# When the accumulator of the first graph layer is zeroed, which engine empties the table's products, and how many buffers that stage has

## The chip, the cores and the metric

The kernel runs on one core of one Trainium2 chip. The core has five engines that run side by side, each with its own queue of instructions: TensorE (PE in the profile, with its weight loads as PEld), VectorE (DVE), ScalarE (ACT), GpSimd (POOL) and SyncE (SP), which mostly issues transfers. ACT, SP and POOL issue DMAs. The time is that of one execution on the device in microseconds (us). Before the change the median of 11 runs is 4143.52 us (4135.31 to 4149.55). The time wanted is the median after the change.

## The reference

Four layers run on a graph with 6250 nodes of 256 features and 100000 edges, sorted by destination: a graph attention block (two attention layers), a mixture of experts, a graph layer with weighted means, and a second mixture of experts. Only the opening of the first attention layer matters here:

```python
x = x + _L0_gnn_ref(_layernorm(x, axis=-1), src, dst, ...)
# gat_layer, first call: 2 heads of 128
z = (x @ W).reshape(num_nodes, heads, d)
el = jnp.einsum('nhd,hd->nh', z, a_l)
er = jnp.einsum('nhd,hd->nh', z, a_r)
...
s = jax.ops.segment_sum(ex, dst, num_segments=num_nodes)
alpha = ex / s[dst]
msg = z[src] * alpha[:, :, None]
out = jax.ops.segment_sum(msg, dst, num_segments=num_nodes)
```

## The kernel before, in words

The 6250 nodes are 50 tiles of 125. A layer on the graph takes the tiles in turn: for each of a tile's 16 groups of 128 edges it gathers the sources' rows from a table in DRAM (`z<-table,src_all`, line 755, an indirect DMA on POOL), and TensorE adds them up by destination (line 946). Sums that belong to edges beyond a tile's 16 groups go through an accumulator in DRAM, `sums1` for the first layer: a few "over" groups are added up first and written to its rows (lines 741 to 748), and each tile adds the rows that it finds there (`old<-sums`, line 663). So `sums1` has to be zero before any of this: 6528 rows of 258 floats, 1032 bytes each, 6.74 MB.

The first stage, lines 1145 to 1184, prepares all that, and the change lies in it. It has these parts, in the order of the program:

- `edge_ranges` (lines 124 to 407) finds where each tile's edges begin and end. It is one chain with three rounds of indirect loads on POOL: the whole edge list is loaded and reduced, then `part` (line 177, 50 rows of 6256 bytes), then `win` (line 220, three loads of 50 rows of 1024 bytes), from which VectorE makes `wd` (line 226), then `orec` and `ow` (line 293, eight loads of 128 small records). Between the rounds stand dozens of small VectorE instructions and small matmuls into a `p` buffer of PSUM, two of which exist. At its end `starts` (line 383) and `shift_held` (line 407) are there.
- `edge_lists` (lines 441 to 499) reads `starts` into registers of SP and POOL and loads each tile's edges and weights in 7 groups of 8 tiles (lines 460 and 463; two buffers), turns them on TensorE and stores them in the lists that the gathers use.
- `gat_weights` prepares `wl`, the layer's weights.
- A loop makes the table in 13 blocks of up to four tiles (lines 1151 to 1173): load `xb` on ACT's queue (three buffers), layer norm on VectorE, turn on TensorE (line 523) and copy on ScalarE (line 524), then per tile four matmul instructions into `pz` (line 1164, two buffers of PSUM). Two engines empty a `pz`: ScalarE its 256 columns of z (line 1168), VectorE its 4 columns of scores (line 1171). Then the rows (two buffers) are stored on ACT's queue (line 1106).
- Some blank rows are stored, `sums1` is zeroed by one DMA on SP's queue from a blank SBUF tile of 128 partitions (`clear`, line 1120), and `item_lists` (lines 409 to 433) makes the list for a loop that handles irregular tiles.

No `manual_schedule` stands around this stage. The framework's scheduler chooses the order in which each engine gets these instructions, from the program's order and its own estimates, and puts the waits in. So an instruction that is ready early is issued early although it stands late in the program: the zeroing of `sums1`, nearly the last line of the stage, is issued 10.93 us after the start. Within an engine the order is then fixed, and an instruction that waits holds all behind it.

After the stage comes the loop for irregular tiles, with a run-time count (line 651); all engines meet there. The first gather of the layer is issued at 169.33 us, and from there the order is written out by hand (lines 967 to 1015).

Of the kernel before, what the change touches and what calls it, by code (L numbers as in the profile page):

```python
# [13 lines left out]
F32 = mybir.dt.float32  # L14
# [4 lines left out]
OP = mybir.AluOpType  # L19
# [8 lines left out]
P = 128  # L28
NP = 125
D = 256  # L30
# [4 lines left out]
TB = 4  # L35
# [9 lines left out]
def network(ctx: ExitStack, tc: tile.TileContext, a, out, n_nodes: int, n_edges: int):  # L45


    nc = tc.nc
    NT = a["x"].shape[0] // NP
# [71 lines left out]
        return t  # L121


    def edge_ranges():

# [1 line left out]
        with tc.tile_pool(name="rng", bufs=1) as pool, tc.tile_pool(  # L129
            name="rng_ps", bufs=2, space=PSUM  # L130
# [60 lines left out]
            p = ps.tile([P, 512], F32, name="p")  # L191
# [32 lines left out]
                )  # L224
            wd = pool.tile([NT, 3 * P], F32, name="wd")
            nc.vector.tensor_copy(wd, win.rearrange("p i e k -> p (i e) k")[:, :, 1])
            nc.vector.tensor_scalar(c(18), c(18), float(P), None, op0=OP.add)
            upper = pool.tile([NT, 3 * P], F32, name="upper")
            nc.vector.scalar_tensor_tensor(
# [9 lines left out]
            p = ps.tile([P, 512], F32, name="p")  # L239
# [7 lines left out]
            p = ps.tile([P, 512], F32, name="p")  # L247
# [20 lines left out]
            p = ps.tile([P, 512], F32, name="p")  # L268
# [50 lines left out]
            p = ps.tile([P, 512], F32, name="p")  # L319
# [6 lines left out]
            p = ps.tile([P, 512], F32, name="p")  # L326
# [20 lines left out]
            p = ps.tile([P, 512], F32, name="p")  # L347
# [22 lines left out]
            p = ps.tile([P, 512], F32, name="p")  # L370
# [10 lines left out]
            p = ps.tile([P, 512], F32, name="p")  # L381
            nc.tensor.matmul(p[:1, :NT], c(5), identf[:NT, :NT], start=True, stop=True)
            nc.vector.tensor_copy(starts, p[:1, :NT])
            p = ps.tile([P, 512], F32, name="p")
# [117 lines left out]
    def normalize(pool, outs, ins, keep=None):  # L502

        n, p = len(ins), ins[0].shape[0]
        mv = keep if keep is not None else pool.tile([P, TB, 2], F32, name="mv")
        for j, x in enumerate(ins):
            st = pool.tile([P, 6], F32, name="st", bufs=4)
            nc.vector.bn_stats(st[:p], x)
            nc.vector.bn_aggr(mv[:p, j, :], st[:p])
        nc.scalar.activation(mv[:p, :n, 1:2], mv[:p, :n, 1:2], AF.Sqrt, bias=eps[:p])  # L510
        nc.vector.reciprocal(mv[:p, :n, 1:2], mv[:p, :n, 1:2])
        for j, (o, x) in enumerate(zip(outs, ins)):
            nc.vector.tensor_scalar(
                o, x, mv[:p, j, 0:1], mv[:p, j, 1:2], op0=OP.subtract, op1=OP.mult
            )

    def transpose_to(xT, ps, ins, func=AF.Copy):

        n, q = len(ins), ins[0].shape[0]
        for k in range(KD):  # L520
            pt = ps.tile([P, TB, P], F32, name="pt")
            for j, x in enumerate(ins):
                nc.tensor.transpose(pt[:, j, :q], x[:, k * P : (k + 1) * P], identf[:q, :q])
            nc.scalar.activation(
                xT[:, k, : n * q].rearrange("p (j q) -> p j q", q=q), pt[:, :n, :q], func
            )


    def gat_width(H):
        return H * (D // H + 1)  # L530

    def gat_weights(pool, W, al, ar, H):

        d = D // H
        wl = pool.tile([P, KD, D + 2 * H], F32, name="wl")
        nc.sync.dma_start(wl[:, :, 0:D], W.rearrange("(k p) f -> p k f", p=P))
        for s, v in enumerate((al, ar)):
            vb = row_to_all(pool, v, f"vb{s}")
            for h in range(H):
                for k in range(KD):  # L540
                    pr = pool.tile([P, D], F32, name="pr", bufs=2)
                    nc.vector.tensor_mul(pr[:, :d], wl[:, k, h * d : (h + 1) * d], vb[:, h * d : (h + 1) * d])
                    nc.vector.tensor_reduce(
                        wl[:, k, D + s * H + h : D + s * H + h + 1], pr[:, :d], AX.X, OP.add
                    )
        return wl
# [550 lines left out]
    def tiles_of(src, t0, n):  # L1097

        w = src.shape[1]
        return bass.AP(tensor=src.tensor, offset=src.offset + t0 * NP * w, ap=[[w, P], [NP * w, n], [1, w]])  # L1100

    def store_tiles(queue, dst, t0, n, v):

        to = dst[t0 * NP : (t0 + n) * NP, :].rearrange("(j p) w -> p j w", p=NP)
        for q in (slice(0, NP // 16 * 16), slice(NP // 16 * 16, NP)):
            queue.dma_start(to[q], v[q])  # L1106
# [7 lines left out]
    def clear(queue, acc, part, parts):  # L1114

        w = acc.shape[1]
        step = -(-NS // parts)
        lo, hi = part * step, min(NS, (part + 1) * step)
        if lo < hi:
            queue.dma_start(  # L1120
                acc[:, :].rearrange("(p j) w -> p j w", p=P)[:, lo:hi, :],
                blank[:, 0:w].unsqueeze(1).to_broadcast([P, hi - lo, w]),
            )
# [12 lines left out]
    x5_d = dram.tile([NT * NP, D], F32, name="x5_d")  # L1136
    uv_d = dram.tile([NT * NP, 2 * D], F32, name="uv_d")
    x6_d = dram.tile([NT * NP, D], F32, name="x6_d")
    NS = -(-(NT * NP + 2 * P) // P)
    sums1 = dram.tile([NS * P, gat_width(2)], F32, name="sums1")  # L1140
    sums2 = dram.tile([NS * P, gat_width(1)], F32, name="sums2")
    sums3 = dram.tile([NS * P, D + 1], F32, name="sums3")


    with tc.tile_pool(name="g1w", bufs=1) as wpool, tc.tile_pool(name="g1", bufs=2) as work, tc.tile_pool(
        name="g1p", bufs=2, space=PSUM
    ) as ps:
        edge_ranges()
        edge_lists()
        wl = gat_weights(wpool, a["L0_gnn_W1"], a["L0_gnn_al1"], a["L0_gnn_ar1"], 2)  # L1150
        for t0, n in blocks:
            xb = work.tile([P, TB, D], F32, name="xb", bufs=3)
            nc.scalar.dma_start(xb[:, :n, :], tiles_of(a["x"], t0, n))
            xb = xb[:NP]
            normalize(work, [xb[:, j, :] for j in range(n)], [xb[:, j, :] for j in range(n)])
            xT = work.tile([P, KD, TB * NP], F32, name="xT")
            transpose_to(xT, ps, [xb[:, j, :] for j in range(n)])
            rows = work.tile([NP, TB, D + 6], F32, name="rows")
            heads = rows[:, :, 0 : D + 2].rearrange("p j (h f) -> p j h f", h=2)
            nc.vector.memset(heads[:, :, :, 0:1], 1.0)  # L1160
            for j in range(n):
                pz = ps.tile([P, 512], F32, name="pz")
                for k in range(KD):
                    nc.tensor.matmul(
                        pz[:NP, : D + 4], xT[:, k, j * NP : (j + 1) * NP], wl[:, k, :],
                        start=(k == 0), stop=(k == KD - 1),
                    )
                nc.scalar.copy(
                    heads[:, j, :, 1:], pz[:NP, 0:D].rearrange("p (h f) -> p h f", h=2)
                )  # L1170
                nc.vector.tensor_copy(rows[:, j, D + 2 :], pz[:NP, D : D + 4])
            nc.vector.tensor_copy(er1[:NP, t0 : t0 + n, :], rows[:, :n, D + 4 :])
            store_tiles(nc.scalar, table1, t0, n, rows[:, :n, :])
        none = wpool.tile([NT + 1, 2 * P], BF16, name="none")
        nc.vector.memset(none, 0.0)
        for v, k in ((er1_d, 6), (er2_d, 3)):
            nc.sync.dma_start(
                v[:, :, CH:, :].rearrange("t k c e -> t k (c e)"),
                none.unsqueeze(1).to_broadcast([NT + 1, k, 2 * P]),
            )  # L1180
        nc.sync.dma_start(x2_d[NT * NP :, :], blank[: P - NP, 0:D])
        nc.sync.dma_start(table3[NT * NP :, :], blank[: P - NP, 0 : D + 1])
        clear(nc.sync, sums1, 0, 1)
        item_lists()
    gat_general(2, table1, er1, sums1, m_all)

# [188 lines left out]
    with tc.tile_pool(name="f1w", bufs=1) as wpool, tc.tile_pool(name="f1x", bufs=3) as work, tc.tile_pool(  # L1375
        name="f1p", bufs=2, space=PSUM
# [17 lines left out]
        rows = wpool.tile([P, NC, 2], I32, name="rows")  # L1394
# [43 lines left out]
        p = ps.tile([P, 512], F32, name="py")  # L1438
# [3 lines left out]
        p = ps.tile([P, 512], F32, name="py")  # L1442
# [88 lines left out]
    with tc.tile_pool(name="f1c", bufs=2) as work:  # L1531
        for t0 in range(0, NT, TL):
# [8 lines left out]
            rows = work.tile([NP, TL, D + 1], F32, name="rows")  # L1541
# [383 lines left out]
    with tc.tile_pool(name="f3w", bufs=1) as wpool, tc.tile_pool(name="f3", bufs=1) as work, tc.tile_pool(  # L1925
        name="f3p", bufs=1, space=PSUM
# [51 lines left out]
```

## Time and profile before

| | us |
|---|---|
| median of 11 runs | 4143.52 |
| the profiled execution, its own time | 4141.28 |
| its span, first to last instruction | 4139.6 |
| first 168 us of it: PE busy | 103.36 |
| first 168 us: DVE busy | 100.09 |
| first 168 us: ACT busy | 41.00 |
| first 168 us: POOL busy | 41.25 |

The profile comes from one execution. The span leaves out 1.7 us of that execution's own time. In lines of the timeline the columns are the start in us, the duration in us, the engine (a q marks its queue, which issues DMAs), the line of the kernel, the operation, output and input, and the number of instructions; in brackets stands how long the engine sat idle before, and what ended that. The lines by window give each engine's busy us and number of instructions, the granted clock of TensorE, the mean busy share of the 16 DMA engines and GB/s.

### The profile page before, as it was taken

The page shows a single profiled execution, that of the slowest core. Times are in us where ns is not written, and L with a number is a line of the kernel's source. Part 1 is how long each engine was busy: PE and PEld are TensorE (multiplying, and loading weights), DVE is VectorE, ACT ScalarE, POOL GpSimd, SP SyncE. Part 2 cuts the span into 40 slices and gives each one's busy share as a digit, 9 for nine tenths or more (in the row PEclk, how much of TensorE's full clock was granted, in tenths as well). Part 3 has the DMA queues.
Part 4 walks back from the last instruction along what each step waited for, and adds up shares of the span by engine and source line. Part 5 has one row for each costly group of instructions (what it writes and reads, how often), then busy time and mean ns, then how long its engine had stood idle before and what let it go on. Part 6 is the DMA issues. An engine that isn't in the chain of part 4 may idle for free. (4 is left out here: it accounts for less than half of the span.)

```text
span 4139.6 us, 38013 instructions
## 1 busy us (share of the span) xinstructions
PE 2873.8 (69%) x11159; PEld 2004.7 (48%) x11159; DVE 2443.3 (59%) x4938; ACT 994.1 (24%) x1877; POOL 2614.8 (63%) x2717
## 2 busy tenths in 40 slices
PE   5556556666645666767667699990788888889854
PEld 3334434444433444444445477760346666666643
DVE  5666666666646777777777333336345445544474
ACT  1222222222212222223222122220011212222243
POOL 2477777777747777777776144440777777777611
PEclk8777878788777888888888699995678999989987
DMA  6445555555535555555554411128454544554644
GB/s 164 140 143 157 165 157 157 156 156 156 157 103 149 163 163 163 163 163 163 164 165 128 143 64 64 65 70 248 126 148 136 150 137 134 147 144 139 165 125 131
DMA packets 323716, 593.10 MB, mean 143 GB/s; under 512 B 64327, under 2 KB 210396, under 8 KB 323247
## 3 DMA queue, kind: packets, MB, share of 16 engines
q0 software_dynamic: 128432, 349.50, 30.2%
q1 hardware_dynamic: 177542, 223.76, 18.8%
q10 hardware_dynamic: 17529, 17.31, 1.4%
q8 instruction: 96, 1.57, 0.2%
q14 instruction: 117, 0.96, 0.1%
HBM read 489.23 MB, written 101.12 MB: 143 GB/s over the span
## 5 line engine op out<-in xcount | busy, mean ns | idle before, releaser
L755 POOL DMA_INDIRECT z<-table,src_all x2412 | 2330.3, 966 | 847.1 <-issue 797.7
L946 PE MATMUL pacc<-z,wt 128*125 128x258 f32 (+1 forms) x3216 | 950.1, 445 | 20.5 <-DVE old L956 17.6
L946 PEld LDWEIGHTS pacc<-z,wt 128*125 128x125 f32 x3216 | 680.0, 222 | 174.4 <-issue 26.2
L1075 PE MATMUL pacc<-z,wt 128*125 128x257 f32 x1608 | 490.9, 446 | 105.1 <-DMA z<-table,src_all 95.5
L895 PE MATMUL pq<-identf,el 128*34 128x128 f32 (+1 forms) x306 | 78.7, 391 | 668.1 <-ACT el L888 569.9
L1075 PEld LDWEIGHTS pacc<-z,wt 128*125 128x125 f32 x1608 | 312.2, 210 | 270.0 <-DMA z<-table,src_all 220.4
L765 DVE TENSOR_TENSOR oh<-iota_b,px 128x2000 bf16<-128x2000 bf16 x153 | 339.7, 2221 | 120.1 <-ACT px L1047 119.9
L895 PEld LDWEIGHTS pq<-identf,el 128*34 128x34 f32 (+1 forms) x306 | 26.4, 112 | 718.5 <-ACT el L888 645.4
L862 ACT CAST e<-pe 6x1536 bf16<-6x1536 f32 (+1 forms) x204 | 203.6, 998 | 688.8 <-PE pe L858 688.6
L934 DVE TENSOR_TENSOR z<-z,pq 128x1032 f32<-128x1032 f32 (+1 forms) x202 | 233.6, 1218 | 179.1 <-PE pq L918 175.6
L846 DVE TENSOR_TENSOR own<-dr,px 125x2048 bf16<-125x2048 bf16 x102 | 232.6, 2281 | 21.1 <-ACT px L844 13.0
L1759 PE MATMUL pt<-x6T,w1f 128*128 128x250 f32 x800 | 187.8, 392 | 69.0 <-ACT hT L1765 69.0
L1512 POOL DMA_INDIRECT y_d<-y,r x105 | 104.4, 994 | 197.6 <-DVE r L1456 171.1
L858 PE MATMUL pe<-own,ek 125*6 125x512 bf16 (+1 forms) x408 | 149.4, 457 | 101.1 <-DVE own L846 88.7
L1482 PE MATMUL ph<-w,xT 128*128 x420 | 201.2, 602 | 13.2 <-DVE xT L1471 7.3
L1759 PEld LDWEIGHTS pt<-x6T,w1f 128*128 128x128 f32 x800 | 157.2, 199 | 93.1 <-ACT hT L1765 74.9
L888 ACT COPY el<-z 128x32 f32<-128x32 f32 (+2 forms) x102 | 23.6, 231 | 739.5 <-DMA z<-table,src_all 716.0
L1506 PE MATMUL py<-w,hT 128*128 x840 | 198.5, 379 | 0.0
L1774 PE MATMUL py<-w2f,hT 128*125 128x256 f32 x800 | 189.4, 397 | 0.0
L899 DVE TENSOR_TENSOR_SCAN f<-mask,pq 34x384 f32<-34x384 bf16 (+1 forms) x100 | 93.8, 938 | 139.5 <-PE pq L895 139.3
L1774 PEld LDWEIGHTS py<-w2f,hT 128*125 128x125 f32 x800 | 159.7, 201 | 26.1
L1506 PEld LDWEIGHTS py<-w,hT 128*128 128x128 f32 x840 | 151.5, 190 | 16.3
(479 smaller groups left out, 3877.8 us busy)
## 6 DMA issues: line engine op xcount, KB each, us to landing
dr<-dl_d SPq DMA_DIRECT2D x102, 512.0 KB
z<-table,src_all POOLq DMA_INDIRECT x2412, 2.8
sums<-blank SPq DMA_DIRECT2D x16, 771.0 KB
uv_d<-uv SPq DMA_DIRECT2D x25, 448.0 KB
z<-uv_d SPq DMA_DIRECT2D x10, 1120.0 KB
old<-sums SPq DMA_DIRECT2D x13, 514.0 KB
sums<-blank SPq DMA_DIRECT2D x1, 6579.0 KB
old<-sums SPq DMA_DIRECT2D x10, 645.0 KB
```

The source lines that it names most:

```text
L755: nc.gpsimd.indirect_dma_start(out=z[:, c, :], out_offset=None, in_=table[:, :], in_offset=bass.IndirectOffsetOnAxis(ap=src_all[:, i : i + ...
L765: nc.vector.tensor_tensor(oh[:, c0:c1], iota_b[:, 0:NP].unsqueeze(1).to_broadcast([P, n, NP]), px[:, c0:c1].unsqueeze(2).to_broadcast([P, ...
L846: nc.vector.tensor_tensor(own, s["dr"][:NP], px[:NP, X : X + 1].to_broadcast([NP, CH * P]), OP.is_equal)
L858: nc.tensor.matmul(pe[:, c - lo : c - lo + n], ek[:, NT if t == OVER else t].rearrange("p i h -> p (i h)"), s["own"][:, c : c + n], start= ...
L862: nc.scalar.copy(s["e6"][:, lo:hi], pe[:, 0 : hi - lo])
L934: nc.vector.tensor_tensor(zz, zz, x.unsqueeze(2).to_broadcast([P, n, d + 1]), OP.mult)
L946: nc.tensor.matmul(s["pacc"][:NP, 0:w], s["wt"][:, c, :], s["z"][:, c, 0:w], start=(c == 0), stop=(c == n - 1),)
L1075: nc.tensor.matmul(pacc[:NP, 0:w], s["wt"][:, c, :], s["z"][:, c, :], start=(c == 0), stop=(c == chunks(t) - 1),)
L1482: nc.tensor.matmul(ph, v["xT"][:, k, :], w1[:, v["one"], k, :].rearrange("p o f -> p (o f)"), start=(k == 0), stop=(k == KD - 1),)
L1506: nc.tensor.matmul(py[:, :D], v["hT"][:, f, :], w2[:, v["one"], f, :].rearrange("p o f -> p (o f)"), start=(f == 0), stop=(f == KF - 1),)
L1759: nc.tensor.matmul(ph[:, g * W : (g + 1) * W], x["w1"][:, s, k, f * P : (f + 1) * P], xT[:, k, :], start=(k == 0), stop=(k == KD - 1),)
L1774: nc.tensor.matmul(py[:NP, s, :], hT[:, s * KF + f, :], x["w2"][:, s, f, :], start=(f == 0), stop=(f == KF - 1),)
```

## The change

`edge_ranges` gets a tile `zeros` of 48 partitions and 258 columns and fills it right after `wd`, by multiplying a part of `wd` with 0. One DMA on SP's queue stores it into all of `sums1`, each partition 136 times; the old zeroing at the end of the stage goes. As it reads `zeros`, this DMA can't be issued before `wd` is known. The 4 columns of scores in `pz` are copied by ScalarE where VectorE did it. The buffers of `xb` go from 3 to 5, those of `rows` from 2 to 3, those of `pz` from 2 to 3.

```diff
-    def edge_ranges():
+    def edge_ranges(zeros):
...
             nc.vector.tensor_copy(wd, win.rearrange("p i e k -> p (i e) k")[:, :, 1])
+            nc.vector.tensor_scalar(zeros, wd[:ZP, : zeros.shape[1]], 0.0, None, op0=OP.mult)
...
+    ZP = 48
     NS = -(-(NT * NP + 2 * P) // P)
+    assert NS * P % ZP == 0 and ZP <= NT
...
-        edge_ranges()
+        zeros = wpool.tile([ZP, gat_width(2)], F32, name="zeros")
+        edge_ranges(zeros)
+        rows_z = NS * P // ZP
+        nc.sync.dma_start(
+            sums1[:, :].rearrange("(p j) w -> p j w", p=ZP), zeros.unsqueeze(1).to_broadcast([ZP, rows_z, zeros.shape[1]])
+        )
         edge_lists()
...
-            xb = work.tile([P, TB, D], F32, name="xb", bufs=3)
+            xb = work.tile([P, TB, D], F32, name="xb", bufs=5)
...
-            rows = work.tile([NP, TB, D + 6], F32, name="rows")
+            rows = work.tile([NP, TB, D + 6], F32, name="rows", bufs=3)
...
-                pz = ps.tile([P, 512], F32, name="pz")
+                pz = ps.tile([P, 512], F32, name="pz", bufs=3)
...
-                nc.vector.tensor_copy(rows[:, j, D + 2 :], pz[:NP, D : D + 4])
+                nc.scalar.copy(rows[:, j, D + 2 :], pz[:NP, D : D + 4])
...
-        clear(nc.sync, sums1, 0, 1)
         item_lists()
```

## The prediction

> **What bounds the kernel now.** I first read the page's busy times, then the windows over the first 168 us, since only that stage changes, then its timeline and its waits.
>
> ```profile
> span 4139.6 us, 38013 instructions
> PE 2873.8 (69%) x11159; PEld 2004.7 (48%) x11159; DVE 2443.3 (59%) x4938; ACT 994.1 (24%) x1877; POOL 2614.8 (63%) x2717
> ...
> 0.00:168.00 168.00, 103.36 (x402) 69.74 (x402) 100.09 (x504) 41.00 (x112) 41.25 (x76) 0.85 0.55 142
> 168.00:4139.60 3971.60, 2770.42 (x10757) 1934.99 (x10757) 2343.16 (x4436) 953.12 (x1766) 2573.59 (x2641) 0.82 0.50 143
> ```
>
> In the first stage no engine is busy for two thirds of the time: PE leads with 103 of 168 us. So it is bound by waits. The other 3971.6 us are ordered by hand and untouched; I count them as unchanged. The timeline of the stage shows one chain from load to load:
>
> ```profile
> 10.93 0.65 SPq L1120 DMA_DIRECT2D sums<-blank  x1
> 15.59 26.10 SPq L1247 DMA_DIRECT2D y_d<-blank  x1
> 17.77 1.34 POOL L177 DMA_INDIRECT part<-in_edges,row  x1 [15.00 <-DVE wl L543]
> 29.17 0.56 DVE L183 CAST pd<-part 50x782 f32<-50x782 int32 x1 [7.09 <-DMA part<-in_edges,row]
> 35.72 0.93 POOL L220 DMA_INDIRECT win<-in_edges,near  x1 [16.61 <-DVE near L217]
> 44.32 0.43 DVE L508 BATCH_NORM_STATS2 st<-xb 125x6 f32<-125x256 f32 x1 [4.88 <-DMA xb<-in_x]
> 45.33 0.34 DVE L226 CAST wd<-win 50x384 f32<-50x384 int32 x1
> 57.91 0.17 DVE L276 COPY over<-p 128x12 f32<-128x12 f32 x1 [2.33 <-PE p L273]
> 60.45 0.97 POOL L293 DMA_INDIRECT orec<-in_edges,at_i  x1 [21.19 <-DVE sl L314]
> 72.54 0.17 DVE L299 TENSOR_SCALAR w_all<-ow 128x4 f32<-128x4 f32 x1 [0.40 <-DMA ow<-in_edge_weight,at_i]
> 84.90 6.76 SPq L460 DMA_DIRECT2D raw<-in_edges  x11
> 139.29 0.37 SPq L495 DMA_DIRECT2D run_d<-nb  x1
> 165.16 0.21 SPq L433 DMA_DIRECT2D item_off<-to  x1
> 169.33 0.97 POOL L755 DMA_INDIRECT z<-table,src_all  x1 [0.30 <-issue]
> ```
>
> The store of 6.74 MB of zeros goes out at 10.93, and the next DMA on SP takes 26.10 us to get past it. Right behind, `part` and `win` are asked for and come late: VectorE idles 7.09 us for the one and, around the other, 4.88 us for a block's `xb`. Then come `orec`, the first edge lists at 84.90, their last store at 139.29, the item lists until 165.16, the layer at 169.33. The DMA view of two windows, 11 to 46 us and 47 to 84 us, tells when the transfers are busy:
>
> ```profile
> DMA packets 8053, 8.34 MB, mean 238 GB/s; under 512 B 188, under 2 KB 7972, under 8 KB 8052
> q1 hardware_dynamic: 6705, 6.77, 89.9%
> ...
> DMA packets 3490, 3.21 MB, mean 87 GB/s; under 512 B 413, under 2 KB 3488, under 8 KB 3488
> ```
>
> SP's queue (q1) moves 6.77 MB in the first 35 us, so the store takes 35 us. In the next 37 us little is moved. The change shifts the store from the first window to the second.
>
> **The change part by part.** All sums are against the profiled execution's own 4141.28 us.
>
> *The store leaves the front.* `part` is issued at 17.77 and used at 29.17, 11.4 us later. Other indirect loads in this stage land 2.8 us (z, 2.1 MB in 16 loads), 3.6 us (`orec`) after issue by the DMA view. `part` is 0.31 MB in one load; I take at most 4.3 us, and then VectorE, busy until 22.07, doesn't wait: **-7.1** (from 0, if the two added `xb` loads of 0.5 MB take the store's place, to -7.1). The three loads of `win` land 6.7 us after issue by the same view; at 2.8 that is **-3.9**. For this the 4.88 us that VectorE waits for `xb` must go too: that load is issued only at 33.02, when a buffer comes free, and competes with the store; with five buffers it is issued among the first. Bounds 0 and -4.9.
>
> *The filling of `zeros`.* One VectorE instruction of 48x258 on the chain. The row of `wd` (50x384) is 0.34: **+0.3**.
>
> *The store in its new place.* It is issued when `wd` is known, at 45.33 + 0.34 + 0.3 - 11.0 = 35.0. The eight `orec` and `ow` loads then run beside it. They are on the chain (VectorE waits 4.83 and 0.40 us for them). `win` lost 3.9 us beside the same store; these move 128 records of 4 or 8 bytes each and are eight in a row of which the last counts. Bounds 0 and +3.9, I take **+2**. It ends at 35.0 + 0.65 + 35 = 70.6. What is queued behind the waiting store on SP: the register loads of `starts` and the edge lists' loads. They waited until 84.90 and come by this sum at 73.9, so there are 3 us between, and as the first group is used 6 us after its first load, 9 us of cover. `sums1` is read first near 239 us. The store's rate isn't known from 48 partitions. From 128 it is 6.74 MB / 35 us = 193 GB/s; were it proportional to the partitions, 72 GB/s and 93 us. I take 35, because the row has the same bytes in the same pieces of 1032 on the same queue.
>
> [...]
>
> *ScalarE empties `pz`.* VectorE loses 50 copies of 0.15, 7.2 us. ScalarE gains 50 copies; its nearest rows are 0.16 (128x16) and 0.20 (128x8), so 8 to 10 us on an engine that is busy for 41 of 168. On the path it matters that PE waits 18.3 us in 11 places for VectorE's copy before it may write `pz`, because VectorE has other work or a wait in front. One such place is on the chain: the matmul of line 273 stands behind those of `pz`, and VectorE waits 2.33 us for it: **-2.3** (0 to -2.3). Sum up to the edge lists: -7.1 - 3.9 + 0.3 + 2 - 2.3 = **-11.0**.
>
> *Five `xb`, three `rows`, three `pz`.* From 84 to 139 VectorE waits 2.69, 1.49 and 0.20 us for `xb`, with the edge lists' instructions behind it: **-3** (0 to -4.4). The rest of the 54 us goes by the lists' own loads, two buffers deep, and stays. From 139.29 to 165.16, 25.9 us, three and a half blocks of the table and the item lists remain, and PE is nearly full (19.2 of 20 us from 140 to 160). A block costs it 2 x 2.02 + 0.91 = 4.95 us. If blocks can run ahead in PE's and VectorE's earlier waits (18.3 and 14.6 us), fewer remain. I take one block: **-4.9** (0 to -9.9).
>
> Sum: -11.0 - 3 - 4.9 = **-18.9**, 4122.4 for an execution like the profiled one. The median of the runs shown is 2.2 us above that execution, so 4124.6; I say **4125**. All best ends give -28.3, 4115.
>
> **The rivals.** About 0.2%, 8.3 us, is what a measurement of this kernel can tell from no change.
>
> 1. *Only the chain moves.* The edge lists keep their pace, the blocks their place between them, the tail its 25.9 us. For it: the lists' waits are mostly for `raw` (9.1 us on ACT). -11.0, **4132.5**, and from 4129 to 4139 with the terms' ends.
> 2. *The table ends the stage, not the chain.* The 13 blocks are stored between 44.84 and 161.48, 9.7 us for each, and the last is 3.7 us before the last item list. If their pace is set by how the scheduler mixes them with the rest, what the chain gains is spent waiting. Against it: PE needs only 4.95 a block. **4142**, a few us to either side. It would also be seen if `part` came no earlier, the added `xb` loads having taken the store's place.
> 3. *The store stands before the edge lists (slower).* The lists' loads are on the same SP queue. With 48 partitions at a proportional rate the store lasts 93 us, to 128.7, and the first group comes near 130 where it was used at 90.9: +39, less the 3 and at most 9.9 of tail whose blocks are done meanwhile: about +26, **4170**. It costs from 44 us on (the 9 us of cover) and turns the sign near 63 us, 107 GB/s. Against it: the 193 GB/s row; for it: nothing in this trace stores much from so few partitions.
>
> **How the numbers follow.** Forecast 0.58, own range 4115 to 4135. Rival 1: 0.17, of it 0.12 faster and 0.05 within 0.2% (above 4135.2). Rival 2: 0.15, within. Rival 3: 0.07, slower; another 0.03 slower for an order of the scheduler's that puts a wait in front of the chain. So faster 0.70, same 0.20, slower 0.10. The range goes from 4112 (the best ends, and 3 us of spread between runs) to 4143, which takes in rival 1 and half of rival 2 and leaves out some 0.18.
>
> **What would show it.** VectorE's wait for `part` near zero and `pd` near 22; `wd` near 34; the store from 35 to 71, and SP's first load of edges near 74, landing without delay; PE's waits for line 1171 gone; the last edge list near 125, the last item list near 146, the first gather near 150. It is wrong if `part` still lands 11 us after issue, if the store lasts beyond 44 us, or if the stage's end stays while the edge lists begin earlier.

## The result, and the profile after

The changed kernel has a median of 4179.28 us in 8 runs (4174.76 to 4190.33); the kernel before, beside it on the same chip, 4144.69 us in 31. The ratio is 1.0087, with a 95% interval from 1.0077 to 1.0096: 0.87% slower, some 36 us by the ratio. The forecast was 4125 us, with a range up to 4143.

The profiled execution after has 4181.36 us of its own. Its page and two windows, cut at the end of the first stage (columns as before):

```profile
span 4179.5 us, 38019 instructions
...
0.00:208.80 208.80, 111.28 (x402) 72.65 (x402) 94.03 (x455) 45.62 (x162) 40.68 (x77) 0.73 0.45 114
208.80:4179.50 3970.70, 2775.74 (x10757) 1941.03 (x10757) 2343.36 (x4436) 953.62 (x1766) 2576.98 (x2641) 0.82 0.50 143
```

What comes after the stage takes 3970.7 us where it took 3971.6. All of the loss lies in the stage, 208.8 instead of 168 us, with hardly more work in it: VectorE is busy for 6 us less, ScalarE for 5 us more. The same places of the timeline after, up to the item lists' last store and the first gather:

```profile
17.84 1.34 POOL L178 DMA_INDIRECT part<-in_edges,row  x1 [15.07 <-DVE wl L545]
22.72 0.56 DVE L184 CAST pd<-part 50x782 f32<-50x782 int32 x1 [0.58 <-DMA part<-in_edges,row]
29.27 0.94 POOL L221 DMA_INDIRECT win<-in_edges,near  x1 [10.10 <-DVE near L218]
34.52 0.35 DVE L227 CAST wd<-win 50x384 f32<-50x384 int32 x1 [0.81 <-DMA win<-in_edges,near]
35.42 0.69 SPq L1155 DMA_DIRECT2D sums<-zeros  x1
42.67 5.73 ACTq L1108 DMA_DIRECT2D table<-rows  x2
47.42 0.97 POOL L295 DMA_INDIRECT orec<-in_edges,at_i  x1 [14.69 <-DVE sl L316]
68.31 0.18 DVE L511 BATCH_NORM_AGGREGATE mv<-st 125x2 f32<-125x6 f32 x1 [16.65 <-DMA table<-rows]
72.01 0.16 DVE L301 TENSOR_SCALAR w_all<-ow 128x4 f32<-128x4 f32 x1
89.54 0.18 DVE L513 RECIPROCAL mv<-mv 125x4 f32<-125x4 f32 x1 [8.41 <-DMA table<-rows]
89.87 0.40 ACTq L1162 DMA_DIRECT2D xb<-in_x  x1
90.76 0.37 ACT L1177 COPY rows<-pz 125x256 f32<-125x256 f32 x1 [14.05 <-PE p L355]
93.62 0.19 DVE L385 CAST starts<-p 1x50 int32<-1x50 f32 x1
96.14 4.49 POOL L465 DMA_DIRECT2D wraw<-in_edge_weight  x8 [39.00 <-PE pz L1173]
111.27 0.82 ACTq L1108 DMA_DIRECT2D table<-rows  x2
115.18 5.09 SPq L462 DMA_DIRECT2D raw<-in_edges  x3
180.04 0.31 SPq L497 DMA_DIRECT2D run_d<-nb  x1
205.94 0.21 SPq L435 DMA_DIRECT2D item_off<-to  x1
210.11 0.97 POOL L757 DMA_INDIRECT z<-table,src_all  x1 [0.30 <-issue]
```

Up to the first `orec` the chain gains 13.0 us (60.45 to 47.42). Then it loses. In us, from one place to the next:

| step | before | after | difference |
|---|---|---|---|
| start to first `orec` | 60.45 | 47.42 | -13.0 |
| to `starts` | 22.8 | 46.2 | +23.4 |
| to SP's first load of edges | 1.6 | 21.6 | +19.9 |
| to the lists' last store | 54.4 | 64.9 | +10.5 |
| to the first gather | 30.0 | 30.1 | 0 |
| sum | 169.33 | 210.11 | +40.8 |

Three kinds of wait are new, or far longer than before. The first: VectorE stands idle for 16.65 and 8.41 us until a *store of the table* has landed: its memset of a block's ones (line 1169) must not overwrite rows that are still being stored, and the program places that wait on the instruction just ahead. The store issued at 42.67 took 5.73 us to issue alone (0.87 before) and was waited for until 68.31. The second: SP's first load of edges waits, though `starts` is known. The waits of SP's queue from 96 to 136 us (us in total, times, longest) name the same transfers:

```profile
SPq L462 <- DMA table<-rows: 27.6, 3, 19.9
```

The loads read nothing that these stores write. The built program tells why they wait: the framework hands eight completion semaphores round among the DMAs of SP and ScalarE, and a DMA waits until the one that had its semaphore before it has landed (it *inherits* the semaphore). For the first load of edges that is the second store of the table's 7th block, issued at 111.27; before it was the 2nd block's first store.

The third wait is ScalarE's, 14.05 us up to 90.76. The view puts it down to a matmul, but by the built program the load of `xb` issued at 89.87, ahead of that copy in ScalarE's program, inherits the semaphore of the store of zeros itself. The trace's record of that semaphore has the store's last completion at 89.8. So ScalarE, and with it the table, stands until the whole store has landed. In the kernel before, that semaphore goes on to a store of the table issued after 61 us, and the zeros had landed at 48.8.

What makes the table's stores slow runs beside them. From 35 to 95 us the DMA view (the row's 40 slices of 1.5 us, then SP's queue) says of after:

```profile
DMA  7999999999999999999887779767665542210370
...
q1 hardware_dynamic: 6544, 6.74, 58.7%
```

The store isn't over in 35 us. It keeps the engines at nine tenths up to 63 us and then drains for over 20 us; by single us, the queue's last packets are near 89, so it lasted **54 us**. The row is a mean over the engines. That parts of the store end far apart the semaphore shows: its sixteen completions come between 63.5 and 89.8 us.

### The profile page after: what moved, and what is told of

Read it like the earlier page. It is cut to its first block, busy times and chain, and to the rows that moved or that the text cites. A ratio compares the mean times of both kernels' runs of the same rounds, so it can differ in the third digit from the quotient of the medians.

```text
span 4179.5 us, 38019 instructions
## 1 busy us (share of the span) xinstructions
PE 2887.0 (69%) x11159; PEld 2013.7 (48%) x11159; DVE 2437.4 (58%) x4889; ACT 999.2 (24%) x1927; POOL 2617.7 (63%) x2717
## 5 line engine op out<-in xcount | busy, mean ns | idle before, releaser
L1767 PEld LDWEIGHTS pt<-x6T,w1f 128*128 128x128 f32 x800 | 157.4, 200 | 94.3 <-ACT hT L1773 76.1
L890 ACT COPY el<-z 128x32 f32<-128x32 f32 (+2 forms) x102 | 23.6, 231 | 720.8 <-DMA z<-table,src_all 710.5
```

The costliest lines, as they stand in the source:

```text
L1767: nc.tensor.matmul(ph[:, g * W : (g + 1) * W], x["w1"][:, s, k, f * P : (f + 1) * P], xT[:, k, :], start=(k == 0), stop=(k == KD - 1),)
```

## The experiments

In the table "length" is the store's, from its issue to its queue's last packets; "blocks" is how many blocks of the table the scheduler put ahead of the first edge list in ScalarE's program; "waits for" names the transfer whose semaphore the first load of edges inherits (table's stores counted, two to a block); "hold" is the time from `starts` to that load; the last two columns are the profiled first gather and the ratio to the kernel before beside it. The kernels marked with * ran on two other chips, where TensorE's clock was granted at 0.77 instead of 0.82: their ratios compare, their first gathers only roughly. The profiled executions of e5, e10 and e13 are 27 to 39 us above the medians of their kernels.

| kernel | store | length | blocks | waits for | starts | hold | first gather | ratio (95%) |
|---|---|---|---|---|---|---|---|---|
| before | 128, front | 37 | 4 | store 3 | 83.3 | 1.6 | 169.3 | 1 |
| after | 48 | 54 | 9 | store 14 | 93.6 | 21.6 | 210.1 | 1.0087 (1.0077-1.0096) |
| e1_store_only | 48 | 51 | 9 | store 11 | 85.3 | 23.2 | 197.2 | 1.0059 (1.0038-1.0079) |
| e2_rest_only | 128, front | 44 | 4 | store 4 | 83.1 | 1.6 | 174.2 | 1.0005 (0.9994-1.0016) |
| e3_store_wide | 128 | 40 | 4 | store 4 | 78.2 | 2.0 | 165.8 | 0.9992 (0.9979-1.0005) |
| e4_store_late | 48, after lists | 52 | 4 | store 4 | 73.3 | 1.7 | 195.9 | 1.0062 (1.0041-1.0083) |
| e5_ones_once * | 48 | 52 | 9 | store 12 | 91.2 | 17.0 | 200.1 | 1.0042 (1.0020-1.0064) |
| e7_wide_ones * | 128 | 40 | 4 | a load of xb | 79.9 | 1.9 | 171.1 | 0.9986 (0.9967-1.0004) |
| e8_z64 * | 64 | 43 | 8 | store 7 | 79.2 | 6.5 | 184.6 | 1.0045 (1.0022-1.0069) |
| e9_z48_rows * | 48 | 52 | 9 | store 14 | 92.7 | 20.6 | 207.9 | 1.0083 (1.0056-1.0110) |
| e10_raw_pool * | 48 | 53 | 9 | (POOL) | 93.2 | 2.5 | 213.1 | 1.0058 (1.0032-1.0084) |
| e11_wide_only * | 128 | 42 | 4 | store 3 | 75.6 | 6.4 | 169.8 | 0.9977 (0.9959-0.9994) |
| e12_split * | 128, in three | | 4 | store 4 | 78.6 | 4.3 | 167.0 | 0.9983 (0.9967-1.0000) |
| e13_z32 * | 32 | 44 | 13 | a load of xb | 79.5 | 38.0 | 213.3 | 1.0048 (1.0030-1.0067) |
| e14_held | 48 | 52 | 4 | store of dl_d | 90.4 | 1.7 | 185.0 | 1.0039 (1.0025-1.0052) |
| e15_wide_late_lists | 128 | 40 | 8 | store 4 | 78.0 | 2.4 | 167.0 | 0.9989 (0.9980-0.9998) |

The diffs are against the changed kernel, that of e12 against the kernel before.

**e1_store_only**, the kernel before with only the store moved:

```diff
-            xb = work.tile([P, TB, D], F32, name="xb", bufs=5)
+            xb = work.tile([P, TB, D], F32, name="xb", bufs=3)
...
-                nc.scalar.copy(rows[:, j, D + 2 :], pz[:NP, D : D + 4])
+                nc.vector.tensor_copy(rows[:, j, D + 2 :], pz[:NP, D : D + 4])
```

(`rows` and `pz` go back too.)

> The kernel before with the store alone moved to its new place, from 48 partitions as in the change; buffers and VectorE's copies as before. Times are worked out from the two traces: before to after the first gather moved from 169.33 to 210.11, +40.8, of it -13.0 up to the first orec, +12.5 from there to starts known, wait on the table's stores included, +8.4 to 10.9 to the last of starts, +19.9 from starts to SP's first load of edges, +10.5 in the edge lists. Theory 1 (the long store alone does it: it slows the table's stores and xb, and VectorE and SP wait for them): nearly all of it stays, first gather 200 to 212, time 4170 to 4182. Theory 2 (the added buffers let more table stores go ahead of the edge lists, and SP's loads wait for those; the store only makes each longer): the 19.9 goes to a few us, first gather 180 to 192, time 4150 to 4165. Theory 3 (the copies and the buffers do it, the store is harmless): the front's gain of 11 to 13 alone is left, first gather near 157, time near 4130.

4169.46 us, +0.59%, first gather 197.2: just below both ranges of theory 1 and above those of theory 2. The store alone does most of it, and the hold of 23.2 us is there with the old buffers, against theory 2.

**e2_rest_only**, the change without the moved store:

```diff
-            nc.vector.tensor_scalar(zeros, wd[:ZP, : zeros.shape[1]], 0.0, None, op0=OP.mult)
...
+        clear(nc.sync, sums1, 0, 1)
         item_lists()
```

> The change without the moved store: zeros from 128 partitions at the very front as in the kernel before, with ScalarE's copies and the added buffers. Theory 1 (the moved store does it all): no loss, the front as before with part 11 us late; what the buffers and copies give by the prediction's terms is -2.3, -3 and -4.9, so 4131 to 4141. Theory 2 (buffers put table stores ahead of the edge lists and that alone costs): the step from starts to SP's first load is still 10 to 20 us instead of 1.6, time 4150 to 4165. Theory 3 (copies and buffers cost by themselves): 4170 or more.

4148.68 us, +0.05%: the buffers and copies neither gain, as theory 1 had it, nor lose. `wd` comes 1.9 us earlier (45.33 to 43.40), the edge lists take 57.6 instead of 54.4 us, the tail 31.9 instead of 30.0. The store at the front lasts 44 us here instead of 37; by the DMA view four loads of `xb` start beside it (11 to 55 us), in before one (11 to 48 us).

**e3_store_wide**, the change with 128 partitions instead of 48:

```diff
-        zeros = wpool.tile([ZP, gat_width(2)], F32, name="zeros")
+        zeros = wpool.tile([P, gat_width(2)], F32, name="zeros")
+        nc.vector.memset(zeros, 0.0)
...
-            sums1[:, :].rearrange("(p j) w -> p j w", p=ZP), zeros.unsqueeze(1).to_broadcast([ZP, rows_z, zeros.shape[1]])
+            sums1[:, :].rearrange("(p j) w -> p j w", p=P), zeros.unsqueeze(1).to_broadcast([P, NS, zeros.shape[1]])
```

> The change with the zeros in 128 partitions instead of 48, the store in the new place all the same, rows of the same 1032 bytes. In the trace after, the store from 48 partitions is issued at 35.4 and its last bytes move at about 88; the kernel before needed 35 us from 128. Theory 1a (any store of 6.7 MB in this place holds up the table's stores, and VectorE's and SP's waits for them hold the chain): the store lasts 40 to 50 us because other transfers run beside it, and 25 to 40 of the 40.8 us stay, time 4163 to 4180. Theory 1b (the 48 partitions are the fault, they reach the DMA engines unevenly and the last ones drain late): the store ends near 72, VectorE's waits of 16.7 and 8.4 us shrink to a few, SP's first load of edges comes near 75 to 85, first gather 155 to 165, time 4127 to 4138. Theory 2 (order of the table's stores ahead of the lists): as 1a unless the built order changes; in the built program fewer table stores stand in front of the lists here (80 instead of 140 ScalarE instructions), so the 19.9 us goes and the 12.5 and 10.9 may stay: time 4148 to 4160.

4141.54 us, 0.08% under the kernel before where the change is 0.87% over: nearest to theory 1b, 3.5 us above its range. The scheduler's order changes with it. The DMA view from 35 to 95 us, and the timeline:

```profile
DMA  8999999999999999899999999520550682396119
```

```profile
78.22 0.19 DVE L385 CAST starts<-p 1x50 int32<-1x50 f32 x1
80.19 1.89 SPq L462 DMA_DIRECT2D raw<-in_edges  x4
```

The engines stay at nine tenths up to 72 us and fall at once; the store's sixteen completions come between 72.6 and 76.1 us. After is later by 15.4 us at `starts`, 19.6 in the hold, 8.8 in the lists and 0.6 in the tail, together the 44.4 us between the two first gathers.

**e4_store_late**, the 48 partitions, issued behind the edge lists:

```diff
-        edge_ranges(zeros)
+        edge_ranges()
+        edge_lists()
+        nc.vector.tensor_scalar(zeros, w_all[:ZP, e_z - zeros.shape[1] : e_z], 0.0, None, op0=OP.mult)
...
-        edge_lists()
```

> The change with the store issued after the edge lists' last stores instead of ahead of them, its zeros taken from the last columns of the weights' table, still 48 partitions. Theory 1 (the store beside table and lists is the fault): the front keeps its gain of 13 us, starts known near 71, first load of edges near 73, last edge list 122 to 128; the store then runs from there beside the item lists and the first gathers, which cost some us more than before. First gather 155 to 170, time 4127 to 4145. Theory 2 (order of the table's stores by the buffers): SP's first load of edges still comes 10 to 20 us after starts, time 4140 to 4160. Theory 3 (copies and buffers cost by themselves): 4165 or more. What would speak against all: the first gathers, which then run beside the store, lose more than 10 us.

4167.82 us: a miss for theory 1, whose front came nearly true (`starts` 73.3, last edge list 130.9), and for the guess that the store would cost little behind it. It is issued at 131.31 and lasts 52 us here too, with 1.3 MB of the table's beside it, so its length isn't the neighbours' doing. The item lists' small stores stand behind it on SP's queue:

```profile
148.61 29.15 SPq L424 DMA_DIRECT2D item_tile<-ti  x1
...
183.49 0.68 DVE L423 TENSOR_SCALAR ti<-p 1x512 int32<-1x512 f32 x1 [27.13 <-DMA item_tile<-ti]
```

A store of 2 KB needs 29.15 us to be issued. The 27 us that VectorE waits for it are more than the whole loss of 22.

**e5_ones_once**, VectorE's wait taken away:

```diff
+        lasting = [wpool.tile([NP, TB, D + 6], F32, name=f"lasting{i}") for i in range(3)]
+        for r in lasting:
+            nc.vector.memset(r[:, :, 0 : D + 2].rearrange("p j (h f) -> p j h f", h=2)[:, :, :, 0:1], 1.0)
...
-            rows = work.tile([NP, TB, D + 6], F32, name="rows", bufs=3)
+            rows = lasting[t0 // TB % 3]
...
-            nc.vector.memset(heads[:, :, :, 0:1], 1.0)
```

> The changed kernel as it is, 48 partitions, but the ones of the table's rows are written once into three lasting tiles instead of before each block, so that VectorE no longer waits for the table's slow stores (16.65 and 8.41 us in the trace after). Theory 1 (VectorE's two waits carry the loss): orec used near 60 instead of 71.5, starts near 72 to 80 instead of 93.62, first load of edges soon after it, first gather 165 to 185, time 4135 to 4155. Theory 2 (the loads of edges are held by the table's stores anyway, in the order the scheduler chose): starts come 12 to 20 earlier, but SP's first load stays at 105 to 115 and the first gather at 195 to 210, time 4165 to 4180.

+0.42%, half of the loss; between the theories. But `starts` comes only at 91.2: with the memset gone, VectorE waits 11.64 us for `orec` itself, whose last load was issued at 53.92 and which is used at 67.66. The indirect loads, too, are late beside this store. That isn't all: from there `starts` takes 23.6 us, against 15.7 in e4. Here the view names the third wait outright:

```profile
88.38 0.16 ACT L1182 COPY lasting<-pz 125x4 f32<-125x4 f32 x1 [12.17 <-DMA sums<-zeros]
```

In front of this copy ScalarE issues a small store of `run_d`, which by the built program inherits the zeros' semaphore; TensorE waits 5.28 us for the copy before it makes its next products, and the matmuls for `starts` stand behind those in TensorE's program.

**e7_wide_ones**, e3 with the ones written once (both diffs).

> The store in the new place from 128 partitions, with the ones written once. In the run with 128 partitions VectorE still waited 5.35 us for a table's store at 54.07, and w_all came at 63.55 where the kernel with the late store had 58.83. If that wait carries it, starts come near 73 instead of 78.22 and the first gather near 161 instead of 165.76: 4135 to 4139 where the kernel before has 4143 to 4146. If the transfers themselves are the limit there, the wait goes to orec or xb and the time stays at 4140 to 4143. If the gain is lost in the table's tail: the same.

0.9986, not told apart from e3's 0.9992. The wait went to `orec` (8.87 us), the second case; ScalarE waits 8.76 us for the zeros here too.

**e8_z64 and e13_z32**, the change with 64 and with 32 partitions (of the 64 only 48 are made from `wd`; a memset zeroes the tile ahead of that), and **e9_z48_rows**, with 48 whose rows are spread over `sums1`:

```diff
-    ZP = 48
+    ZP = 64
...
-    ZP = 48
+    ZP = 32
...
-            sums1[:, :].rearrange("(p j) w -> p j w", p=ZP), zeros
+            sums1[:, :].rearrange("(j p) w -> p j w", p=ZP), zeros
```

> The changed kernel with the zeros in 64 partitions instead of 48. Measured so far: 6.74 MB from 48 partitions last 52 us (with little beside them in the late store, and likewise in the early one), from 128 partitions 40 us beside the table's transfers and 35 in the kernel before. Theory 1 (each partition gives a fixed rate, 6.74 MB / 48 / 52 us = 2.7 GB/s): 64 partitions last 39 us, as long as 128, and the loss goes as far as the order of the table's stores allows. [...] Time: 4140 to 4165 by 1 and 2, 4175 by 3; the built program puts more of the table's stores ahead of the lists than with 128 partitions, so some of the loss may stay in the step from starts to SP's first load.

> The changed kernel with 48 partitions, but each partition's rows are spread over sums1 (row j x 48 + p) instead of lying together. Theory 1 (the partitions that are read are the limit): the store lasts 50 to 55 us as before and the time is 4175 to 4183. Theory 2 (the place in memory that is written is the limit, 48 long stretches): the store lasts 35 to 45 us and the time falls by 10 us or more.

> The changed kernel with the zeros in 32 partitions instead of 48. Measured: 48 partitions 52 us with a drain of over 20 us in which engines fall idle one after the other, 64 partitions 41 us and 128 partitions 40 us with a sharp end. Theory 1 (a fixed rate for each partition, 2.7 GB/s): 78 us, the time far over the changed kernel's, 1.2% or more over before. [...]

The DMA view from 35 to 95 us, of 64 and of 32 partitions:

```profile
DMA  8899999999999999999999999973017393117528
```

```profile
DMA  9499999999999999999999999996301721930481
```

Both end sharply, after 43 and 44 us: the row falls from nine tenths to nothing within 4.5 us, where in after it takes over 20. **32 partitions are faster than 48** (44 us against 51 to 54), so it isn't a fixed rate for each partition (78 us). Nor is it where the zeros are written: spread over memory they take the same 52 us and cost the same 0.83%. That leaves an uneven spread of the 48, my assumption in theory 2 of both. The measured ends agree with it: from 48 the parts end far apart, the completions of after over 26.3 us, and from 64 and 32 nearly together by the rows. Theory 3 of e8 had its 4175 from a store of 50 us or more; it lasted 43. What is uneven in a store from 48 partitions no run shows, nor what limits the others: 32 and 64 take hardly longer (44 and 43 us) than 128 in this place (40 to 42 us).

The times of both are 0.45% and 0.48% over before all the same. The short store doesn't bring the order back: 8 and 13 blocks of the table stand ahead of the first edge list, and the hold is 6.5 and 38 us. In e8 the first load is only the first of several that wait for the table (SP's queue, from `starts` to the lists' last store):

```profile
SPq L462 <- DMA table<-rows: 16.7, 5, 5.2
```

The fewer the partitions, the more blocks, although the chip is faster with 32 than with 48 (44 us against 51 to 54): the scheduler seems to go by an estimate of its own; that was read from the built orders alone.

**e10_raw_pool**, the loads of edges on POOL's queue:

```diff
-                    nc.sync.dma_start(
+                    nc.gpsimd.dma_start(
                         raw[s], a["edges"][bass.ds(off, G), :].rearrange("(c p) k -> c p k", p=P)
                     )
```

> The changed kernel as it is, with the edge lists' loads of edges issued by POOL instead of SP, so that they wait for no transfer of SP's or ScalarE's queue. In the trace after, starts were known at 93.62, POOL's loads of weights went out at 96.14 and SP's loads of edges at 115.18, held for 19.9 us by the table's stores. Theory 1 (that hold is a loss of its own): the first load of edges goes out at 96 to 102, the first gather comes 10 to 20 us earlier than 210, so 0.4% to 0.6% over the kernel before instead of 0.87%; POOL then issues two loads where it issued one, which may take a few us of it back. Theory 2 (the table's stores fill the engines, and the lists would come late by any queue): the loads land as late as before, first gather 205 to 212, 0.8% to 0.9% over.

Inconclusive. The profiled execution has

```profile
95.76 0.56 POOL L462 DMA_DIRECT2D raw<-in_edges  x1 [39.50 <-PE pz L1173]
...
133.78 0.31 ACT L469 CAST sf<-raw 128x128 f32<-128x128 int32 x1
```

The load goes out 19.4 us earlier than in after and the first list is copied as late as in after, at 133.82 there. That copy stands behind 9 blocks in ScalarE's program, and most of them stand behind the store's end. The first gather is late as in theory 2. But the six executions fall into two groups, four at 4829 to 4836 us and two at 4868 to 4872 (before: 4810.74), and the profile is of the second. What the first did differently isn't known.

**e11_wide_only**, e1 with the 128 partitions of e3, and **e12_split**, which stores them in three pieces:

```diff
+        for lo, hi, z in ((0, 16, blank[:, : zeros.shape[1]]), (16, 34, zeros), (34, NS, zeros2)):
+            if z is zeros2:
+                nc.vector.tensor_scalar(zeros2[:125], w_all[:125, NT * CH : NT * CH + 1].to_broadcast([125, zeros.shape[1]]), 0.0, None, op0=OP.mult)
+            nc.sync.dma_start(to_z[:, lo:hi, :], z.unsqueeze(1).to_broadcast([P, hi - lo, zeros.shape[1]]))
```

> The kernel before, its buffers and copies, with the store alone moved and from 128 partitions. From 48 partitions the same edit cost 0.59%. Theory 1 (the 48 partitions are the whole fault, moving is a gain): part at 22.7, orec issued near 49, starts near 75 to 79, first load of edges 2 us later, first gather 155 to 165, 0.1% to 0.3% faster than before. Theory 2 (the store in the new place costs as much as it gives, whatever its width): within 0.1% of before. Theory 3 (the gain with 128 partitions came from the buffers): slower than before by 0.1% or more.

> The kernel before, its buffers and copies, with the zeros stored from 128 partitions in three pieces where the queue is little used: 2.1 MB at the start, 2.4 MB when the edges of the tiles are known, 2.2 MB when the last orec has been used. The kernel with the late store showed what the chain does with no store beside it: starts at 73.3, first load of edges at 75, last list at 131. If the store's company is what the wide store still costs, starts come at 73 to 76 and the first gather at 155 to 161: 0.2% to 0.3% faster than before. If the front piece delays part or win again, or the last piece the lists, it is no better than the single wide store: within 0.1% of it.

e11 is 0.9977, faster than both kernels with its whole interval under 1: theory 1. `starts` comes at 75.6. The split is 0.9983, no better: the piece at the front delays `part` again (used at 27.10 instead of 22.7).

**e14_held and e15_wide_late_lists** set the order apart from the length. e14 keeps 48 partitions and holds two blocks of the table behind the first list; e15 keeps 128 and puts the lists behind nine blocks in the program:

```diff
+            if t0 // TB in (4, 5):
+                nc.vector.tensor_scalar(
+                    heads[:, :, :, 0:1], dl_all[:NP, 0 : 2 * TB].rearrange("p (j h f) -> p j h f", h=2, f=1), 0.0, 1.0, op0=OP.mult, op1=OP.add
+                )
...
-        edge_lists()
...
         for t0, n in blocks:
+            if t0 // TB == 9:
+                edge_lists()
```

> The changed kernel, store from 48 partitions, with the order of the table's blocks given back by a dependence: the ones of blocks 4 and 5 are made from the first edge lists (0 x list + 1), so that 4 blocks stand ahead of the first edge list in every engine's program, as in the kernel before, where the change has 9. Theory 1 (the order that the scheduler chose carries the loss): 0.1% to 0.4% over the kernel before, where the change was 0.83% to 0.87% over; in the profile the first edge list's copy stands within 15 us of its loads' landing. Theory 2 (the length and the drain of the store itself carry it): 0.6% or more. Half and half would give 0.4% to 0.6%.

> The other side: the store from 128 partitions, which cost nothing (0.08% under the kernel before, 4 blocks ahead of the first edge list), but with the edge lists put into the program behind nine blocks, so that 8 blocks stand ahead of the first list. Nothing is added or left out. Theory 1 (the order carries the loss): 0.4% to 0.7% over the kernel before, with a store as short as 40 us. Theory 2 (the store's length carries it): within 0.15% of the kernel with the wide store, so from 0.25% under to 0.1% over.

Of e14 the timeline, and of e15 SP's wait for the table (from `starts` to the lists' last store, as for e8 above):

```profile
88.42 0.16 ACT L1185 COPY rows<-pz 125x4 f32<-125x4 f32 x1 [12.89 <-DMA sums<-zeros]
90.41 0.20 DVE L385 CAST starts<-p 1x50 int32<-1x50 f32 x1
92.09 1.38 SPq L462 DMA_DIRECT2D raw<-in_edges  x3
```

```profile
SPq L462 <- DMA table<-rows: 1.2, 2, 0.8
```

e14 loses 0.39%: the hold is gone, more than half of the loss with it, and `starts` is as late as with any store from 48 partitions; VectorE's wait for the table has gone with the memset of these blocks, and ScalarE's wait for the zeros is in its place. That is half and half, not theory 1. e15 refutes theory 1 as I put it: 8 blocks ahead of the first list cost nothing (0.9989). So their number alone isn't it. What sets e15 apart from the orders that lose is which transfer SP's loads wait for. In e15 that is store 4, long landed. In after it is store 14, in e1 11, in e9 14, in e5 12, in e8 7, in e13 a late load of `xb`, and in each of these SP's first load is held for 6.5 to 38 us, by the table or `xb`. In all others the table holds it for no more than about 2 us (in e11's 6.4 and e12's 4.3 us most of the wait is for the small store of `run_d`). That this wait carries the order's part of the loss is argued from the kernels side by side, not shown by itself, and the profile of e10, where the load goes out early and the first list is no earlier, speaks against the first load alone.

So the cause is the source of 48 partitions: with 128 and the rest as it was, the loss is gone (e3 beside the change, e11 beside e1). It works in two ways. It makes the store 52 us long on the chip; what runs beside it, indirect loads and the table's stores, comes late, and what inherits its semaphore on ScalarE's queue waits for its end: `starts` at 85 to 94 us instead of 76 to 80. And it makes the scheduler place more of the table ahead of the lists, so that SP's loads inherit semaphores of late stores. e14 gives the first some 0.4% and the second some 0.5%, roughly, since its added dependence may cost something itself. Open stays how the first divides between slow neighbours and the zeros' own semaphore, how the second divides between SP's waits and ScalarE's order, and how much of the lists' own +10.5 us belongs to which.

## Why the prediction was wrong, point by point

- **The store leaves the front: right.** `wd` comes 10.8 us earlier, `pd` near 22 and `wd` near 34 as forecast, and the store is issued at 35.42 where 35.0 was worked out. **ScalarE empties `pz`: right** as far as the chain goes; `orec` gains 2.2 us more, where -2.3 was taken (e2, with the copies and buffers but the old store, has 13.06 us from `wd` to `orec` where before has 15.12).
- **"I take 35, because the row has the same bytes in the same pieces": wrong.** This is the step that failed first. The row was of 128 partitions (37 us by its last packets), and the number of partitions was what changed: 52 us with little beside it (e4), 51 to 54 in the new place, 40 to 42 there from 128.
- **"They are on the chain … I take +2": wrong in what it counted.** I looked for who runs beside the store and named `orec` and `ow`. The table's stores run beside it too, and VectorE waits for them ahead of the chain's instructions; and ScalarE's queue waits for the store itself, through its semaphore, 12.2 us in e5 and 12.9 in e14. From the first `orec` to `starts` the step grew by 23.4 us, not 2. Without a store beside it (e4) `starts` comes at 73.3, with a wide one at 75.6 to 79.9: even a wide one costs 2 to 7 us here.
- **"9 us of cover": wrong.** I asked what is queued behind the store on SP and held that the lists' loads would follow it at 73.9. The store's place on SP's queue wasn't what held them. A semaphore shared with the table's stores did, for 21.6 us, and this can't be seen in the trace of before, where the load inherits a store that landed long ago. "An order of the scheduler's that puts a wait in front of the chain" had 0.03.
- **"Five `xb`, three `rows`, three `pz`", -3 and -4.9: wrong, both are nought** (e2 +0.05%, its lists and tail longer). The tail isn't the table: in after the table's last store goes out at 162.76, before the edge lists' last at 180.04, and the tail is still 30.1 us. It is the item lists' own chain, 25.9 us from the edge lists' last store to theirs, before and after.
- **Rival 3** had the sign, nearly the time (4170) and half of the reason, the store's length from 48 partitions. That its time came so near is luck: it took 93 us for the store and let the lists stand behind it on SP's queue. Measured were 54 us, and waits that it didn't have. Its turning point, 63 us, was too late, as it reckoned with the queue of SP alone.
- Even with 128 partitions the change would have been worth 0.08% (e3, not told apart from nothing), and with the store alone 0.23% (e11), not the 0.46% that I forecast.

## What to carry to other kernels

A row of the same bytes isn't a row of the same transfer: if the number of partitions changes, take the length of a transfer as unknown between far bounds: the 6.74 MB here took 40 to 42 us from 128 partitions and 51 to 54 from 48 in the same place. A larger count isn't always faster: here 48 partitions were slower than 32 (44 us). When a long transfer is moved, list every transfer that will run beside it and whoever waits for those, not only what is queued behind it. And when a transfer's shape changes, look in the built program for which earlier DMAs the loads of the critical chain wait for, and which DMA inherits the semaphore of the long transfer: in both places a stranger can stand.

## What the runs showed that I had not expected

- 6.74 MB in pieces of 1032 bytes took 37 to 44 us from 128 partitions (40 to 42 in the new place), 43 from 64, 44 from 32 and 51 to 54 from 48. From 48 the sixteen completions were 26 us apart (after), from 128 in the new place 3.5 us (e3).
- A DMA waited for a transfer that it had nothing to do with, by an inherited semaphore: SP's load of edges 21.6 us for the table's, ScalarE's store of `run_d` 12 to 13 us for the zeros.
- Behind or beside such a store small things waited long: a 2 KB store took 29.15 us to issue on the same queue (e4), and a pair of the table's stores 5.73 us on another (after; 0.87 before).
- The scheduler put 13 blocks of the table ahead of the first list for 32 partitions, 9 for 48, 8 for 64 and 4 for 128, against the chip between 32 and 48; the order that comes with 32 and 64 goes with a loss of 0.45% to 0.48% although the store is nearly as short as from 128.
